# Deformable convolution in a hybrid block: gathering both neighbours of a sampling point from one long row instead of from a table of pairs

## The chip, the cores and the metric

The kernel runs on one core of a Trainium2 chip. The metric is the device time of one execution in microseconds (us). The core has the engines PE (TensorE), DVE (VectorE), ACT (ScalarE), POOL (GpSimd) and SP (SyncE, which here only issues DMAs). DMAs are issued from the instruction queues of SP, ACT and POOL, and an issue that waits holds up whatever stands behind it in that queue.

## The reference, cut to what matters

Four images of 64 x 64 tokens with 256 channels go through a deformable convolution, an additive attention and a routed feed-forward. The change is in the convolution's sampling. Every token has, for each of 8 groups of 32 channels and each of 9 taps, an offset; at that place the projected image `xp` is read by bilinear interpolation of four corners, weighted with a softmax mask, and summed over the taps.

```python
out = corner(x0i, y0i, (1.0 - fx) * (1.0 - fy))
out = out + corner(x0i + 1, y0i, fx * (1.0 - fy))
out = out + corner(x0i, y0i + 1, (1.0 - fx) * fy)
out = out + corner(x0i + 1, y0i + 1, fx * fy)
...
m = mask.reshape(N, H * W, G, P).transpose(0, 2, 1, 3).reshape(N * G, 1, H * W, P)
out = (samples * m).sum(-1)
...
return out @ out_w + out_b
```

## The kernel before

**Near and far tokens.** Most offsets are below 1 in size. For these tokens the sampling is a small dense product: a window of 5 x 5 weights for each token, written to DRAM, laid out as a band, turned on PE and multiplied with the projected rows of a tile of 16 x 8 tokens. Tokens with a larger offset are far tokens. Up to 128 of each image are listed (`list_tokens`) and computed exactly, one token to a partition, in `exact_rows`; an image with more than 128 would take another path (`sample_any`), which is not entered here.

**The table of pairs.** The projected rows are stored in DRAM as `xt_d`, one row of 256 channels for each position of the padded image (66 positions to a line). For the far tokens there is a second table `tab_d`: for each position and each group its 32 channels and the 32 channels of the next position, 64 numbers or 256 bytes. `pairs(i)` makes it: SP loads 128 positions with their right neighbours from `xt_d` (L471), ACT copies them into the order of groups (L476), ACT stores them (L477). It is called 33 times for each image, from `projection`, which evicts the projected rows on ACT (L458) and stores them (L460). Before all this, `zm`, a tile of zeros, is stored to the edges of `xt_d` and `tab_d` and to the four bands (L1625, L1630), and the pool of `zm` is closed before the next stage's tiles are allocated.

**Far tokens.** `exact_rows` is a generator. It fetches the offsets and masks of the listed tokens, computes the positions `ti` and the weights `wg`, and then, for each of 8 groups, issues 18 indirect DMAs on POOL (9 taps and 2 lines, L728), one for 128 tokens, two of them in each step. Then come one multiplication on DVE with the weights (L739, 1152 elements to a partition) and two reductions over the taps and corners (L742, 576 elements each). The tile `ga` has one buffer, so the next group's gathers wait for these reductions. The multiplication stands three steps after the last gather.

**Stages and order.** The first stage runs the convolution's offsets and weights for all four images, in 32 slabs of 512 tokens (`offsets_and_weights`); from slab 4 on, the sampling of image 0 (`sample_image(0, 3)`) goes along with it, and from slab 9 on its far tokens. A slab has five places at which sampling advances, by two, two, two, two and one steps. Then follow four rounds of preparation, feed-forward of the image before, and attention. Attention of image n has 256 steps, and at each of them the sampling of image n + 1 advances by one step, its far tokens too. One step of sampling is one entry of an order of 227: four transposes of weights (drained on DVE as `wt`, L817), a product (`ac`, L836) or an output (`xr`, L850), and at each new tile the loads of its rows and the addition `xr` on POOL (L806). `next(single)` adds to each step one piece of `exact_rows`. The order of the instructions on PE, DVE and POOL is that of the program where `keep` stands around them: here for the gathers, the multiplications and reductions, and the sampling's own instructions. In an attention step POOL also does `s12` (L1219) and `s3a` (L1221), whose sum DVE adds up at L1223 and L1226; there is one L1226 in each step.

Of the kernel before, what the change touches and what calls it, by code (L numbers as in the profile page):

```python
# [10 lines left out]
F32 = mybir.dt.float32  # L11
# [12 lines left out]
G, K2 = 8, 9  # L24
GP = G * K2
# [26 lines left out]
def layers_kernel(ctx: ExitStack, tc: tile.TileContext, a, out: bass.AP):  # L52
# [6 lines left out]
    def scratch(name, shape, dtype=F32):  # L59
        return [nc.dram_tensor(f"{name}{n}", shape, dtype, kind="Internal").ap() for n in range(NB)]  # L60

    tab_d = scratch("tab", [NPOS * G, 2 * CG])
    xt_d = scratch("xt", [NPOS, C])
    raw_d = scratch("raw", [L, 3 * GP])
    wc_d = scratch("wc", [L, RUN])
# [205 lines left out]
    def offsets_and_weights(images, slab):  # L271
# [163 lines left out]
        def image(at):  # L435
# [2 lines left out]
            xn = xns.pop(n)  # L438


            tabw = tab_d[n].rearrange("(q g) c -> q (g c)", g=G)

            def projection(s):

                for i in range(8 * s, 8 * s + 8 + s // 3):
                    if i == 8 * s + 4:
                        yield
                    o = PITCH + i * P
                    pm = S.a_m.tile([P, C], F32, tag="pm", name="pm")
                    for k in range(CC):  # L450
                        pe.matmul(
                            pm, xn[:, k].rearrange("p r q -> p (r q)")[:, o : o + P], inw[:, k, :],
                            start=(k == 0), stop=False,
                        )
                    m = o % PITCH
                    pe.matmul(pm, inside[:, m : m + P].bitcast(R32), inb2.bitcast(R32), start=False, stop=True)
                    xt = S.a_ld.tile([P, C], F32, tag="xt1", name="xt1", bufs=3)
                    nc.scalar.copy(xt, pm)  # L458
                    q0 = LEAD + PITCH + o
                    nc.scalar.dma_start(out=xt_d[n][q0 : q0 + P], in_=xt)  # L460
                    if i > 1:
                        pairs(i - 2)
                if s == 3:
                    pairs(i - 1)
                    pairs(i)

            def pairs(i):

                q0 = LEAD + 2 * PITCH + i * P
                x2 = S.a_ld.tile([P, 2, C], F32, tag="x2", name="x2", bufs=3)  # L470
                nc.sync.dma_start(  # L471
                    out=x2.rearrange("p c e -> p (c e)"),
                    in_=bass.AP(xt_d[n].tensor, xt_d[n].offset + q0 * C, [[C, P], [1, 2 * C]]),
                )
                tb = S.a_ld.tile([P, G, 2, CG], F32, tag="tb", name="tb", bufs=2)
                nc.scalar.copy(tb.rearrange("p g c e -> p c g e"), x2.rearrange("p c (g e) -> p c g e", g=G))  # L476
                nc.scalar.dma_start(out=tabw[q0 : q0 + P], in_=tb.rearrange("p g c e -> p (g c e)"))  # L477

            x1s, raws = {}, {}

# [184 lines left out]
    def exact_rows(n, uf, out_rows):  # L665

        ui = S.smp.tile([P, 1], I32, tag="ui", name="ui")  # L670
        nc.vector.tensor_copy(ui, uf)
        rf = S.smp.tile([P, 1], F32, tag="rf", name="rf")
        nc.vector.tensor_scalar(rf, uf, float(L - 1), None, ALU.min)
        ri = S.smp.tile([P, 4], I32, tag="rii", name="rii")
        nc.vector.tensor_copy(ri[:, 0:1], rf)
        nc.vector.tensor_scalar(rf, rf, float(n * L), None, ALU.add)
        nc.vector.tensor_copy(ri[:, 1:2], rf)
        nc.vector.tensor_scalar(ri[:, 2:3], ri[:, 0:1], W - 1, None, ALU.bitwise_and)
        nc.vector.tensor_scalar(ri[:, 3:4], ri[:, 0:1], 6, None, ALU.logical_shift_right)
# [24 lines left out]
        gt = S.dn.tile([P, 2, GP], F32, tag="gtt", name="gtt")  # L704
        nc.vector.tensor_copy(ti, pos)
        nc.vector.tensor_copy(fl, ti)
        nc.vector.tensor_tensor(gt, fl, pos, ALU.is_gt)
        nc.vector.tensor_sub(fl, fl, gt)
        nc.vector.tensor_sub(pos, pos, fl)
        nc.vector.scalar_tensor_tensor(gt[:, 0], fl[:, 1], float(PITCH), fl[:, 0], ALU.mult, ALU.add)  # L710
        nc.vector.scalar_tensor_tensor(gt[:, 0], gt[:, 0], float(G), gi, ALU.mult, ALU.add)
        nc.vector.tensor_scalar(gt[:, 1], gt[:, 0], float(G * PITCH), None, ALU.add)
        nc.vector.tensor_copy(ti, gt)
        yield True

        wg = S.dn.tile([P, GP, 2, 2], F32, tag="wg", name="wg")
        nc.vector.tensor_mul(fl[:, 1], rw[:, 2 * GP :], pos[:, 1])
        nc.vector.tensor_sub(fl[:, 0], rw[:, 2 * GP :], fl[:, 1])
        for dy in range(2):
            nc.vector.tensor_mul(wg[:, :, dy, 1], fl[:, dy], pos[:, 0])  # L720
            nc.vector.tensor_sub(wg[:, :, dy, 0], fl[:, dy], wg[:, :, dy, 1])

        so = S.dn.tile([P, G, CG], F32, tag="so", name="so")
        for g in range(G):
            ga = S.dn.tile([P, K2, 2, 2, CG], F32, tag="ga", name="ga")
            for s in range(K2):
                for dy in range(2):
                    keep(nc.gpsimd.indirect_dma_start(  # L728
                        out=ga[:, s, dy].rearrange("p c e -> p (c e)"), out_offset=None, in_=tab_d[n],
                        in_offset=bass.IndirectOffsetOnAxis(  # L730
                            ap=ti[:, dy, s * G + g : s * G + g + 1], axis=0
                        ),
                    ))
                yield
            yield
            yield True
            gf = ga.rearrange("p s r c e -> p s (r c) e")
            wv = wg.rearrange("p (s g) r (c o) -> p g s (r c) o", g=G, o=1)[:, g]
            keep(nc.vector.tensor_tensor(gf, gf, wv.to_broadcast([P, K2, 4, CG]), ALU.mult))  # L739
            for e in (slice(0, CG // 2), slice(CG // 2, CG)):  # L740
                yield True
                keep(nc.vector.tensor_reduce(  # L742
                    so[:, g, e], ga[..., e].rearrange("p s r c e -> p e (s r c)"), AX.X, ALU.add,
                ))
            yield
        pt = S.ps_m.tile([P, CC, P], F32, tag="pm", name="pso")
        sof = so.rearrange("p g e -> p (g e)")
# [870 lines left out]
    with scope(("one", 1, 0)):  # L1618
# [1 line left out]
        zm = S.one.tile([P, 2 * HALF * G], F32, name="zm")  # L1620
        nc.gpsimd.memset(zm, 0.0)
        for n in range(NB):
            for d, width in ((xt_d[n].rearrange("q c -> (q c)"), 1), (tab_d[n].rearrange("q c -> (q c)"), 2)):
                for o in (0, (LEAD + (H + 2) * PITCH) * C):
                    nc.scalar.dma_start(  # L1625
                        out=d[o * width : (o + edge) * width].rearrange("(p c) -> p c", p=P),
                        in_=zm[:, : edge * width // P],
                    )
        for slot in band_d:
            nc.scalar.dma_start(out=slot, in_=zm)  # L1630

# [91 lines left out]
```

## Time and profile before

| | |
|---|---|
| three runs | 9395.73, 9403.02 (median), 9404.38 us |
| the profiled execution | 9400.16 us, span 9398.4 us, granted PE clock 0.935 of full speed |
| busy in the span | PE 8133.7 us (87%), DVE 7332.7 (78%), ACT 7317.0 (78%), POOL 5164.1 (55%) |
| DMA traffic | 1282.92 MB, of these 54.39 MB by POOL's queue |
| attention passes (first to last L1133) | 1309 to 3011, 3375 to 5096, 5455 to 7175, 7503 to 9137 us |
| far tokens of image 0, first gather to last reduction | 392 to 845 us |

The profile is of one execution. A line of instructions is named by its line in the kernel. In a table of waits a row says who waited for whom, the sum in us, how often, and the longest. In the groups, the two numbers after the bar are the busy time in us and the mean duration of one instruction in ns; after the next bar stands the idle time of the engine before these instructions, with what ended most of it. A timeline row has the start, the duration, engine, line, operation and tiles. "SPq" and "ACTq" are the queues that issue DMAs.

### The profile page before, as it was taken

The page shows a single profiled execution, that of the slowest core. Times are in us where ns is not written, and L with a number is a line of the kernel's source. Part 1 is how long each engine was busy: PE and PEld are TensorE (multiplying, and loading weights), DVE is VectorE, ACT ScalarE, POOL GpSimd, SP SyncE. Part 2 cuts the span into 40 slices and gives each one's busy share as a digit, 9 for nine tenths or more (in the row PEclk, how much of TensorE's full clock was granted, in tenths as well). Part 3 has the DMA queues.
Part 4 walks back from the last instruction along what each step waited for, and adds up shares of the span by engine and source line. Part 5 has one row for each costly group of instructions (what it writes and reads, how often), then busy time and mean ns, then how long its engine had stood idle before and what let it go on. Part 6 is the DMA issues. An engine that isn't in the chain of part 4 may idle for free. (4 is left out here: it accounts for less than half of the span.)

```text
span 9398.4 us, 119496 instructions
## 1 busy us (share of the span) xinstructions
PE 8133.7 (87%) x35978; PEld 5811.0 (62%) x35978; DVE 7332.7 (78%) x13074; ACT 7317.0 (78%) x8469; POOL 5164.1 (55%) x3124
## 2 busy tenths in 40 slices
PE   5767679999998679999998679999996789999995
PEld 3545447777776357777776357777774456666663
DVE  6777759998987459888887469898987278888872
ACT  3333369999997369999997479999996399999982
POOL 0132057776665357776664367766663456666652
PEclk9888879999999799999998799999998899999997
DMA  5666665554442545554543455554433433333322
GB/s 169 192 187 199 197 204 138 140 136 135 134 135 85 181 133 139 135 136 137 147 119 106 168 132 138 137 144 139 137 112 106 160 116 106 105 102 104 102 85 82
DMA packets 1606155, 1282.92 MB, mean 137 GB/s; under 512 B 128834, under 2 KB 1412068, under 8 KB 1605476
## 3 DMA queue, kind: packets, MB, share of 16 engines
q1 hardware_dynamic: 1433316, 999.33, 36.5%
q10 hardware_dynamic: 139712, 221.19, 6.4%
q0 software_dynamic: 32448, 54.39, 3.9%
q8 instruction: 299, 4.90, 0.2%
q14 instruction: 380, 3.11, 0.1%
HBM read 979.60 MB, written 322.58 MB: 139 GB/s over the span
## 5 line engine op out<-in xcount | busy, mean ns | idle before, releaser
L1133 DVE TENSOR_TENSOR r<-nn,r 128x512 f32<-128x512 f32 x6144 | 4124.3, 687 | 819.0 <-PE nn L1110 605.3
L1219 POOL TENSOR_TENSOR r<-r 128x1024 f32<-128x1024 f32 x1024 | 2706.7, 2643 | 1797.2 <-DVE r L1133 1418.5
L1110 PE MATMUL nn<-qf,kf 128*128 128x512 f32 x8192 | 3227.6, 442 | 243.0 <-DVE r L1133 98.1
L1213 ACT ACTIVATE r<-d 128x1024 f32<-128x1024 f32 x3072 | 3063.7, 1015 | 361.5 <-DVE r L1223 194.4
L1215 ACT ACTIVATE r<-r 128x1024 f32<-128x1024 f32 x3072 | 3132.8, 1055 | 32.5
L1110 PE MATMUL d<-qf,kf 128*128 128x512 f32 x8192 | 2556.1, 414 | 130.9 <-DMA kf<-k 100.6
L1110 PEld LDWEIGHTS nn<-qf,kf 128*128 128x128 f32 x8192 | 1454.0, 188 | 1240.3 <-DVE r L1133 956.2
L1156 PE MATMUL pv<-v,et 128*128 128x257 f32 x8192 | 2134.7, 384 | 18.7 <-DVE acv L1178 18.7
L1110 PEld LDWEIGHTS d<-qf,kf 128*128 128x128 f32 x8192 | 1500.7, 189 | 469.0 <-ACT r L1213 114.1
L1156 PEld LDWEIGHTS pv<-v,et 128*128 128x128 f32 x8192 | 1530.2, 190 | 322.2 <-DVE acv L1178 25.1
L1221 POOL TENSOR_TENSOR r<-r 128x512 f32<-128x512 f32 x1024 | 1334.4, 1303 | 90.0 <-DVE r L1133 10.4
L1223 DVE TENSOR_TENSOR r<-r 128x512 f32<-128x512 f32 x1024 | 729.7, 713 | 19.3 <-POOL r L1219 18.9
L1226 DVE TENSOR_TENSOR et<-r 128x512 f32<-128x512 f32 x1024 | 717.3, 700 | 11.4 <-POOL r L1221 8.0
L728 POOL DMA_INDIRECT ga<-tab,tii x576 | 597.5, 1037 | 146.2 <-issue 114.3
L1140 ACT ACTIVATE et<-et 128x512 f32<-128x512 f32 x1024 | 628.8, 614 | 22.3 <-DVE et L1226 22.3
L806 POOL TENSOR_TENSOR xr<-xr,outb 128x256 f32<-128x256 f32 x128 | 104.0, 813 | 970.5 <-DMA xr<-in_x_dram 622.4
L813 PE MATMUL ptq<-ident,wq 128*120 128x128 f32 x2048 | 327.1, 288 | 149.4 <-DVE ac L836 73.8
L813 PEld LDWEIGHTS ptq<-ident,wq 128*120 128x120 f32 x2048 | 298.2, 185 | 213.0 <-DVE ac L836 63.4
L817 DVE COPY wt<-ptq 120x512 f32<-120x512 f32 x512 | 345.6, 681 | 1.6 <-PE ptq L813 1.5
L1536 POOL DMA_INDIRECT sort<-v,rif x128 | 125.9, 984 | 293.3 <-DVE rif L267 176.6
L476 ACT COPY tb<-x 128x512 f32<-128x512 f32 x132 | 80.3, 615 | 255.0 <-DMA tab<-tb 84.3
L267 PE MATMUL pc<-xn,diag 128*128 128x512 f32 x576 | 260.0, 606 | 8.3 <-ACT xn L413 8.3
(350 smaller groups left out, 5859.7 us busy)
## 6 DMA issues: line engine op xcount, KB each, us to landing
kf<-k SPq DMA_DIRECT2D x4096, 128.0 KB
wq<-band SPq DMA_DIRECT2D x256, 480.0 KB
x<-xt SPq DMA_DIRECT2D x132, 256.0 KB
tab<-tb ACTq DMA_DIRECT2D x132, 256.0 KB
v<-t SPq DMA_DIRECT2D x64, 512.0 KB
k<-kh ACTq DMA_DIRECT2D x128, 256.0 KB
qf<-q SPq DMA_DIRECT2D x256, 128.0 KB
qf<-n SPq DMA_DIRECT2D x256, 128.0 KB
```

What stands on the lines that cost most here:

```text
L728: keep(nc.gpsimd.indirect_dma_start(out=ga[:, s, dy].rearrange("p c e -> p (c e)"), out_offset=None, in_=tab_d[n], in_offset=bass.Indirect ...
L813: keep(nc.tensor.transpose(pt[:HALF, g, :], wq[:, 4 * f + g, :], ident))
L1110: keep(nc.tensor.matmul(dst, ks[b][:, blk, :].bitcast(R32), moving, start=(i == 0), stop=(i == len(blocks) - 1)))
L1133: keep(nc.vector.tensor_tensor(r[:, j, :], nn, r[:, j, :], ALU.mult))
L1140: keep(nc.scalar.activation(ets[b], ets[b], AF.Exp))
L1156: keep(nc.tensor.matmul(pv, ets[b0 + i][:, rows(j)], v[:, k0 + i, :], start=(i == 0), stop=(i == PVB - 1)))
L1213: keep(nc.scalar.activation(rs[b, p], ds.pop((b, p)), AF.Ln))
L1215: keep(nc.scalar.activation(rs[b, p], rs[b, p], AF.Exp, scale=-1.0))
L1219: keep(nc.gpsimd.tensor_tensor(rs[b, 1], rs[b, 1], rs[b, 2], ALU.add))
L1221: keep(nc.gpsimd.tensor_tensor(rs[b, 1][:, 0], rs[b, 1][:, 0], rs[b, 3][:, 0], ALU.add))
L1223: keep(nc.vector.tensor_add(rs[b, 1][:, 1], rs[b, 1][:, 1], rs[b, 3][:, 1]))
L1226: keep(nc.vector.tensor_add(et, rs[b, 1][:, 0], rs[b, 1][:, 1]))
```

## The change

The table of pairs goes: `tab_d`, its zero fills, `pairs` and its calls. `exact_rows` gathers from `xt_d`, seen as rows of 32 channels (position times 8 plus group, the same index as before). Each gather now takes 9 such rows in a run, 288 numbers or 1152 bytes to a token: the first is the group at the position, the last is the group at the next position, and the seven between belong to other groups and are not read. The tile `ga` holds three taps instead of nine, so each group is done in three chunks of six gathers; each chunk has one multiplication and one reduction, into one of three partial sums `so`, and at the end one reduction adds the three. The reduction and the first two gathers of the next chunk are in the same step; the multiplication stands two steps after the last gather. The weights `wg` are laid out by group.

```diff
-    tab_d = scratch("tab", [NPOS * G, 2 * CG])
...
-                    if i > 1:
-                        pairs(i - 2)
-                if s == 3:
-                    pairs(i - 1)
-                    pairs(i)
-
-            def pairs(i):
...
-        wg = S.dn.tile([P, GP, 2, 2], F32, tag="wg", name="wg")
+        wg = S.dn.tile([P, G, K2, 2, 2], F32, tag="wg", name="wg")
...
-        so = S.dn.tile([P, G, CG], F32, tag="so", name="so")
+        so = S.dn.tile([P, 3, C], F32, tag="so", name="so")
+        line = xt_d[n].rearrange("q (g e) -> (q g) e", g=G)
         for g in range(G):
-            ga = S.dn.tile([P, K2, 2, 2, CG], F32, tag="ga", name="ga")
-            for s in range(K2):
-                for dy in range(2):
-                    keep(nc.gpsimd.indirect_dma_start(
-                        out=ga[:, s, dy].rearrange("p c e -> p (c e)"), out_offset=None, in_=tab_d[n],
-                        in_offset=bass.IndirectOffsetOnAxis(
-                            ap=ti[:, dy, s * G + g : s * G + g + 1], axis=0
-                        ),
-                    ))
+            for c in range(3):
+                ga = S.dn.tile([P, 3, 2, G + 1, CG], F32, tag="ga", name="ga")
+                for s in range(3):
+                    for dy in range(2):
+                        j = (3 * c + s) * G + g
+                        keep(nc.gpsimd.indirect_dma_start(
+                            out=ga[:, s, dy].rearrange("p c e -> p (c e)"), out_offset=None, in_=line,
+                            in_offset=bass.IndirectOffsetOnAxis(ap=ti[:, dy, j : j + 1], axis=0),
+                        ))
+                    yield
                 yield
-            yield
-            yield True
-            gf = ga.rearrange("p s r c e -> p s (r c) e")
-            wv = wg.rearrange("p (s g) r (c o) -> p g s (r c) o", g=G, o=1)[:, g]
-            keep(nc.vector.tensor_tensor(gf, gf, wv.to_broadcast([P, K2, 4, CG]), ALU.mult))
-            for e in (slice(0, CG // 2), slice(CG // 2, CG)):
-                yield True
+                gf = ga.rearrange("p s r c e -> p (s r) c e")[:, :, :: G]
+                wv = wg[:, g, 3 * c : 3 * c + 3].rearrange("p s r (c o) -> p (s r) c o", o=1)
+                keep(nc.vector.tensor_tensor(gf, gf, wv.to_broadcast([P, 6, 2, CG]), ALU.mult))
+                yield
                 keep(nc.vector.tensor_reduce(
-                    so[:, g, e], ga[..., e].rearrange("p s r c e -> p e (s r c)"), AX.X, ALU.add,
+                    so[:, c, CG * g : CG * (g + 1)], gf.rearrange("p s c e -> p e s c"), AX.XY, ALU.add
                 ))
-            yield
+        yield
+        sof = S.dn.tile([P, C], F32, tag="sof", name="sof")
+        keep(nc.vector.tensor_reduce(sof, so.rearrange("p c e -> p e c"), AX.X, ALU.add))
+        yield
         pt = S.ps_m.tile([P, CC, P], F32, tag="pm", name="pso")
...
-            for d, width in ((xt_d[n].rearrange("q c -> (q c)"), 1), (tab_d[n].rearrange("q c -> (q c)"), 2)):
-                for o in (0, (LEAD + (H + 2) * PITCH) * C):
...
+            for o in (0, (LEAD + (H + 2) * PITCH) * C):
```

More of the change, by code (lines that the diff above doesn't have):

```diff
@@ L438, in image @@
             xn = xns.pop(n)
-            tabw = tab_d[n].rearrange("(q g) c -> q (g c)", g=G)
             def projection(s):
@@ L460, in projection @@
                     nc.scalar.dma_start(out=xt_d[n][q0 : q0 + P], in_=xt)
-                    if i > 1:
-                        pairs(i - 2)
-                if s == 3:
-                    pairs(i - 1)
-                    pairs(i)
-            def pairs(i):
[L469 to L477, printed above, removed]
             x1s, raws = {}, {}
@@ L714, in exact_rows, with by_tap @@
         yield True
-        wg = S.dn.tile([P, GP, 2, 2], F32, tag="wg", name="wg")
+        wg = S.dn.tile([P, G, K2, 2, 2], F32, tag="wg", name="wg")
         nc.vector.tensor_mul(fl[:, 1], rw[:, 2 * GP :], pos[:, 1])
         nc.vector.tensor_sub(fl[:, 0], rw[:, 2 * GP :], fl[:, 1])
+        def by_tap(t):
+            return t.rearrange("p (s g) -> p s g", g=G)
         for dy in range(2):
-            nc.vector.tensor_mul(wg[:, :, dy, 1], fl[:, dy], pos[:, 0])
-            nc.vector.tensor_sub(wg[:, :, dy, 0], fl[:, dy], wg[:, :, dy, 1])
@@ L723, in exact_rows @@
-        so = S.dn.tile([P, G, CG], F32, tag="so", name="so")
-        for g in range(G):
-            ga = S.dn.tile([P, K2, 2, 2, CG], F32, tag="ga", name="ga")
-            for s in range(K2):
-                for dy in range(2):
-                    keep(nc.gpsimd.indirect_dma_start(
-                        out=ga[:, s, dy].rearrange("p c e -> p (c e)"), out_offset=None, in_=tab_d[n],
-                        in_offset=bass.IndirectOffsetOnAxis(
-                            ap=ti[:, dy, s * G + g : s * G + g + 1], axis=0
-                        ),
-                    ))
-                yield
-            yield
-            yield True
-            gf = ga.rearrange("p s r c e -> p s (r c) e")
-            wv = wg.rearrange("p (s g) r (c o) -> p g s (r c) o", g=G, o=1)[:, g]
-            keep(nc.vector.tensor_tensor(gf, gf, wv.to_broadcast([P, K2, 4, CG]), ALU.mult))
-            for e in (slice(0, CG // 2), slice(CG // 2, CG)):
-                yield True
+            w1, w0 = (wg[:, :, :, dy, dx].rearrange("p g s -> p s g") for dx in (1, 0))
@@ new lines, in exact_rows @@
+            nc.vector.tensor_mul(w1, by_tap(fl[:, dy]), by_tap(pos[:, 0]))
+            nc.vector.tensor_sub(w0, by_tap(fl[:, dy]), w1)
+        so = S.dn.tile([P, 3, C], F32, tag="so", name="so")
+        line = xt_d[n].rearrange("q (g e) -> (q g) e", g=G)
+        for g in range(G):
+            for c in range(3):
[8 more added lines that the diff above has]
+                    yield
+                yield
+                gf = ga.rearrange("p s r c e -> p (s r) c e")[:, :, :: G]
+                wv = wg[:, g, 3 * c : 3 * c + 3].rearrange("p s r (c o) -> p (s r) c o", o=1)
+                keep(nc.vector.tensor_tensor(gf, gf, wv.to_broadcast([P, 6, 2, CG]), ALU.mult))
+                yield
@@ L742, in exact_rows @@
                 keep(nc.vector.tensor_reduce(
-                    so[:, g, e], ga[..., e].rearrange("p s r c e -> p e (s r c)"), AX.X, ALU.add,
+                    so[:, c, CG * g : CG * (g + 1)], gf.rearrange("p s c e -> p e s c"), AX.XY, ALU.add
                 ))
-            yield
+        yield
+        sof = S.dn.tile([P, C], F32, tag="sof", name="sof")
+        keep(nc.vector.tensor_reduce(sof, so.rearrange("p c e -> p e c"), AX.X, ALU.add))
+        yield
         pt = S.ps_m.tile([P, CC, P], F32, tag="pm", name="pso")
-        sof = so.rearrange("p g e -> p (g e)")
@@ L1622, in layers_kernel @@
         for n in range(NB):
-            for d, width in ((xt_d[n].rearrange("q c -> (q c)"), 1), (tab_d[n].rearrange("q c -> (q c)"), 2)):
-                for o in (0, (LEAD + (H + 2) * PITCH) * C):
[L1625 to L1628, printed above, removed]
+            for o in (0, (LEAD + (H + 2) * PITCH) * C):
+                nc.scalar.dma_start(
+                    out=xt_d[n].rearrange("q c -> (q c)")[o : o + edge].rearrange("(p c) -> p c", p=P),
+                    in_=zm[:, : edge // P],
+                )
         for slot in band_d:
```

## The prediction

> **What bounds the kernel now.** I read the page first: four long attention passes, where PE, DVE and ACT are all near 90%, and a first stage where none is.
>
> ```profile
> PE   5767679999998679999998679999996789999995
> DVE  6777759998987459888887469898987278888872
> ```
>
> Each digit is a slice of 235 us. The first five are the convolution stage. The sums by stage give the measure:
>
> ```profile
> 0.00:1250.00 1250.00, 842.70 (x3934) 582.88 (x3935) 913.28 (x1694) 461.49 (x689) 222.26 (x256) 0.82 0.62 191
> 1420.00:3040.00 1620.00, 1553.09 (x7360) 1153.72 (x7360) 1430.06 (x2403) 1502.04 (x1674) 1092.84 (x636) 0.99 0.47 128
> ```
>
> Stretch, length, then busy time of PE, PEld, DVE, ACT, POOL, clock, DMA share. In the first stage ACT is idle 63% of the time and DVE is the busiest; in attention DVE, ACT and PE share the bound. So ACT copies removed from the first stage are not worth their busy time; the question is who waits for them. Next the two groups that the change is about, and who holds SP's queue before 1250 us:
>
> ```profile
> L728 POOL DMA_INDIRECT ga<-tab,tii x576 | 597.5, 1037 | 146.2 <-issue 114.3
> L476 ACT COPY tb<-x 128x512 f32<-128x512 f32 x132 | 80.3, 615 | 255.0 <-DMA tab<-tb 84.3
> ...
> SPq L471 <- DMA xt<-xt: 191.8, 78, 11.2
> ...
> SPq L471 <- ACT tb L476: 40.0, 12, 9.6
> ```
>
> The pairs hold SP for 232 us and ACT idle for 255. Then what DVE waits for while image 0's far tokens are gathered (392 to 846 us):
>
> ```profile
> DVE raw L267 <- PE po L267: 42.4, 22, 5.0
> DVE ga L739 <- DMA ga<-tab,tii: 40.3, 6, 10.4
> DVE ga L739 <- issue: 15.6, 2, 9.0
> ```
>
> No ACT and no pair is in it: DVE waits for the gather itself, 55.9 us before its eight multiplications. In the three attentions the same line waits for nothing.
>
> **The change, part by part.** All sums are against the profiled execution, 9400.2 us (span 9398.4), 2.9 us below the median 9403.02. A difference under 0.2% (19 us) can't be told from none.
>
> *Start: -6 us.* The timeline of the first 50 us:
>
> ```profile
> 37.20 3.60 ACTq L1630 DMA_DIRECT2D band<-zm  x4
> 49.15 0.39 SPq L79 DMA_DIRECT2D inw<-in_L_conv_in_w_dram  x1
> ```
>
> From 29.1 us ACT issues 16 zero fills and the four bands; nothing runs until they have landed at 49.1 and free their buffer. 8 x 134 + 8 x 268 + 4 x 960 KB in 20 us; the 8 x 268 that go are 30% of it, 6.1 us. By issue time alone 8 x 0.47 = 3.8. I take 6; all that follows moves with it.
>
> *132 loads, ACT copies and stores of pairs: -9 us.* Busy time 80 us on ACT, 132 x 0.33 of issue there, but these count only where DVE or PE wait for ACT. From 120 us on, DVE waits for ACT 8.9 us in all (hat 5.1 + 1.2, red 1.5, omax 1.1); behind 0.6 us copies and waits for tab stores stand exactly these activations. So 9. Ends: 0 (they are late anyway) and 25 (PE's 27 us without a named releaser before wq and xw are late loads from SP's queue, and most of that goes too).
>
> *End of the stage: -3 us.* At 1113.9 DVE waits 3.2 us for a position count that is queued on PE behind projections which wait for ACT. The last pair's store is issued at 1149.97, while DVE ends the stage at 1150.1: beside it. 0 to 8.
>
> *DVE work: +5 us in image 0, +11 in the others.*
>
> ```profile
> L739 DVE TENSOR_TENSOR ga<-ga,wg 128x1152 f32<-128x1152 f32 x32 | 46.0, 1437 | 55.9 <-DMA ga<-tab,tii 40.3 <-issue 15.6
> L742 DVE TENSOR_REDUCE so<-ga 128x16 f32<-128x576 f32 x64 | 74.4, 1163 | 0.0
> ```
>
> Now 120.4 us / 4 = 30.1 per image. The multiplication becomes 24 of 384 elements; from 467 ns for 288 (w<-w,mxy) and 1359 for 1152 it is 170 + 1.03 x 384 = 0.57 us. The reduction becomes 24 of 384, all at strides; from 670 ns for 288 (red) and 1160 for 576 it is 0.83. One more sums 768 to 256: at those rates 1.5 to 1.7. 24 x 1.40 + 1.6 = 35.2: +5 per image. In image 0 DVE is the bound: 1 for 1. In attention a step (one sum, L1226, each) takes 6.76, 6.84 and 6.80 us while gathering (intervals of that line, 1420:2060, 3500:4130, 5580:6210) and 6.62, 6.58 and 6.59 after it: 0.21 x 112 steps = 23 us for 30.1 us of DVE, 0.77. 5 x 0.77 x 3 = 11. Ends: 0, if the smaller pieces fit the slack (a step without sampling is 6.24), and 24.
>
> *Gathers: +46 us, all in image 0.* Their number stays 576. A row of 1152 bytes is nowhere in the trace; the nearest, 1024 bytes (xre, L688), takes 0.99 us on POOL and lands in 3.7 to 4.0 us, against 0.95 and 3.4 / 4.0 / 7.9 for 256 bytes. I take no change; the ends are 0.3 us less on the landing and 3.9 more, the slowest gather of now. The Trainium skill (DMA: Bandwidth & Descriptors, Anatomy of one DMA) gives a gather a fixed 2.0 us and its bytes at 436 GB/s: 147 KB against 33 would be 0.26 us more, an estimate, 3 us over the short chunks below; no run here shows it yet.
>
> What moves is the wait. Now a group has 18 gathers in 9 steps, and its multiplication stands three steps after the last. Afterwards a chunk has 6 gathers in 3 steps; the multiplication stands two steps behind, and the next chunk's first gather, in the same step as the reduction, waits for it (one buffer ga). So there is a loop: reduction, gathers, landing, multiplication, with four steps from reduction to multiplication. DVE is in order: behind the waiting multiplication stand the drains wt, ac, xr that PE's next transposes wait for, and the convolution. How long are four steps? The drains tell, one a step:
>
> ```profile
> 924.28 0.28 DVE L836 COPY ac<-pmq 128x128 f32<-128x128 f32 x1
> 924.48 0.41 DVE L850 TENSOR_TENSOR xr<-poq,xr 128x256 f32<-128x256 f32 x1
> 927.17 0.29 DVE L836 COPY ac<-pmq 128x128 f32<-128x128 f32 x1
> 927.37 0.69 DVE L817 COPY wt<-ptq 120x512 f32<-120x512 f32 x1
> 933.19 1.28 DVE L817 COPY wt<-ptq 120x512 f32<-120x512 f32 x2
> 936.83 0.68 DVE L817 COPY wt<-ptq 120x512 f32<-120x512 f32 x1
> 937.43 0.28 DVE L836 COPY ac<-pmq 128x128 f32<-128x128 f32 x1
> 940.07 0.42 DVE L850 TENSOR_TENSOR xr<-poq,xr 128x256 f32<-128x256 f32 x1
> 954.92 0.28 DVE L836 COPY ac<-pmq 128x128 f32<-128x128 f32 x1
> ```
>
> Nine steps come in a burst of 16 us, then 15 us pass. From the nine starts four steps take 8.9, 9.4, 9.6, 10.0, 6.9, 21.0, 18.3, 20.7 and 18.6 us. The loop needs 0.83 + 5 x 1.38 (1.08 and 0.30 of issue) + 4.0 = 11.7. Chunks of 5 steps meet all nine phases, so 5 in 9, 13 of 24, are short, by 2.7 us on average: 36 us. That is the least: in POOL's order between the gathers also stands one addition xr (L806) in every 7 steps, which waits for its load, and POOL idled 207 us before 12 of them in this window. The most: each of the 24 waits as long as the eight do now, 55.9 / 8 = 7.0: 168. Neither is nearer; I take the middle, 102, +46 against 55.9. Ends: -20 and +112. SP without pairs loads xr earlier, which is why I don't go to the upper end.
>
> In attention steps are regular. The last gather of a group landed 13 us or more before its multiplication; one step less leaves 6. The first pair of a chunk now waits for the reduction, so the next s12 (L1219) starts about 1 us later in one step of five; its reader on DVE comes 2 us after it, so I take nothing.
>
> Sum: -6 - 9 - 3 + 5 + 11 + 46 = +44: 9444 against 9400.2, 9447 on the median.
>
> **The rivals.** *Faster:* the gathers find their time. With SP free of 232 us of pair waits, xr comes early, the additions no longer hold POOL, and the waits fall to the least, 36: the term is -20, the sum -22, and with 25 for late loads -38: 9365 to 9385. It decides below 58 us of waits in all (sum zero), 4.5 us for each short chunk. For it: 207 us of POOL idling before that addition. Against it: its load also waits for the store of the tile before, from the drain on DVE, which the pairs don't touch. *Long rows land late:* 24 multiplications each 3.9 us later add 94 us: about 9540. Against it the 1024-byte row. *The row is not one transfer:* if a row of 288 were split at the 32 elements that the index counts in, POOL would have nine times the descriptors; even at half the cost for each, 576 x 4 us of POOL are over 1000 us slower.
>
> **How the numbers follow.** Forecast 0.60: its own range is 9400 to 9520, of which 0.50 lies slower and 0.10 within 0.2%. Faster rival 0.28: 0.17 faster, 0.11 same (its smaller gains). Late rows 0.09 and split rows 0.03: slower. Faster 0.17, same 0.21, slower 0.62. All low ends together give 9348, all high ends 9542; together they are unlikely, so 9375 to 9525.
>
> **What would show it.** Right: the first input load at 43 us instead of 49; no x<-xt on SP; ga lands as before; DVE's wait before L739's successor in image 0 near 100 us, none in attention; image 0's last reduction later than now (845 us), the first attention starting some 30 us later than 1309, steps with gathers near 6.8. Wrong: waits below 58 us, gathers over 1.1 us on POOL, or a change within attention above 24 us.

## The result and the profile after

The changed kernel takes 9450.59 us (median of 5 runs, 9437.30 to 9454.67) against 9404.38 for the kernel before in the same runs: ratio 1.0044, 95% interval 1.0030 to 1.0059, or 46 us slower. The profiled execution took 9437.30 us with a span of 9435.6, 37 us above the profiled one of before. It is the fastest of the five, so the account of the waits below covers 37 of the 46 us.

The page's row of DVE and its DMA line, for the changed kernel (a digit is a slice of 236 us):

```profile
DVE  7766859999997459998987469998987378888872
...
DMA packets 1576204, 1277.57 MB, mean 135 GB/s; under 512 B 124482, under 2 KB 1407716, under 8 KB 1575524
```

The third and fourth digits, 7 and 7 before, are 6 and 6: the first stage has become emptier on its busiest engine, just where image 0's far tokens are gathered. The traffic as a whole is the same, since the longer rows add what the table saved. The sums by stretch, same columns and stretches as before:

```profile
0.00:1250.00 1250.00, 834.03 (x3897) 579.73 (x3898) 903.54 (x1707) 376.74 (x547) 211.01 (x252) 0.81 0.45 138
1420.00:3040.00 1620.00, 1564.97 (x7420) 1153.78 (x7418) 1464.94 (x2440) 1529.45 (x1702) 1115.90 (x650) 1.00 0.52 139
```

ACT lost 85 us of work in the first stage, and DVE did less in the same time, so the stage is stretched by waits. The start, from the timeline:

```profile
33.14 3.24 ACTq L1616 DMA_DIRECT2D band<-zm  x4
44.26 0.39 SPq L78 DMA_DIRECT2D inw<-in_L_conv_in_w_dram  x1
```

The first input load comes 4.9 us earlier. The groups of the gathers (before, then after) and of DVE's two steps:

```profile
L728 POOL DMA_INDIRECT ga<-tab,tii x576 | 597.5, 1037 | 146.2 <-issue 114.3 <-DVE so L742 6.9 <-DMA xr<-in_x_dram 0.3
```

```profile
L717 POOL DMA_INDIRECT ga<-xt,tii x576 | 621.0, 1078 | 381.2 <-DVE so L727 229.7 <-issue 106.3 <-DVE ac L823 24.0
...
L727 DVE TENSOR_REDUCE so<-ga 128x32 f32<-128x384 f32 x96 | 77.6, 808 | 0.0
...
L725 DVE TENSOR_TENSOR ga<-ga,wg 128x384 f32<-128x384 f32 x96 | 54.7, 570 | 120.3 <-DMA ga<-xt,tii 119.3 <-issue 1.0
```

POOL now idles 230 us for the reduction, where before it was 6.9, and DVE idles 120.3 us for gathers instead of 55.9. All of that DVE wait is in image 0. The table of waits while image 0's far tokens are gathered, now 381 to 921 us, and under it the row of before for PE's products (392 to 850 us):

```profile
POOL xr L793 <- DMA xr<-in_x_dram: 177.2, 15, 24.8
...
DVE ga L725 <- DMA ga<-xt,tii: 119.3, 16, 14.7
...
POOL ga L717 <- DVE so L727: 111.2, 15, 18.4
PE pmq L815 <- DVE wt L804: 58.9, 12, 12.2
```

```profile
PE pmq L828 <- DVE wt L817: 18.5, 11, 3.0
```

Read together they are one chain, which the experiments below test: POOL stands before the addition and before the reduction, so DVE stands before its multiplication, and PE's products stand for `wt`, which is queued on DVE behind that multiplication (its longest wait 12.2 us, before 3.0).

What one bad chunk looks like, in the timeline of POOL:

```profile
555.45 0.94 POOL L717 DMA_INDIRECT ga<-xt,tii  x1 [7.31 <-DVE so L727]
556.69 0.95 POOL L717 DMA_INDIRECT ga<-xt,tii  x1 [0.30 <-issue]
578.19 0.72 POOL L793 TENSOR_TENSOR xr<-xr,outb 128x256 f32<-128x256 f32 x1 [20.55 <-DMA xr<-in_x_dram]
579.06 0.96 POOL L717 DMA_INDIRECT ga<-xt,tii  x1
580.33 0.95 POOL L717 DMA_INDIRECT ga<-xt,tii  x1 [0.30 <-issue]
581.58 0.95 POOL L717 DMA_INDIRECT ga<-xt,tii  x1 [0.30 <-issue]
582.83 0.95 POOL L717 DMA_INDIRECT ga<-xt,tii  x1 [0.30 <-issue]
592.97 0.94 POOL L717 DMA_INDIRECT ga<-xt,tii  x1 [9.20 <-DVE so L727]
```

The chunk waits for the reduction, issues two gathers, stands 20.55 us behind the addition `xr` whose load is late, issues its other four, and DVE's multiplication of this chunk waits 14.7 us. Such an addition falls between the gathers of 7 of the 24 chunks. These 7 have 57.4 us of DVE's waits, 8.2 each; the other 17 have 62.9, 3.7 each.

By DVE's account up to the first attention (idle before each of its tiles, before against after), the stage grew from 1309.4 to 1342.4 us: gathers +64.4; the start (`inb`) -5.2; `hat`, `omax` and `red`, which wait for ACT, -8.5; `st`, `oh` and `fl`, all at the end of the stage, -11.7; `raw` -3.9; busy time -0.4; others -1.7. From there on the span is 4.2 us longer (8093.2 against 8089.0), and the three passes with sampling are together 1.9 us longer.

### The profile page after: what moved, and what is told of

It is laid out like the page before. It is cut to its first block, busy times and chain, and to the rows that moved or that the text cites. A ratio compares the mean times of both kernels' runs of the same rounds, so it can differ in the third digit from the quotient of the medians.

```text
span 9435.6 us, 119357 instructions
## 1 busy us (share of the span) xinstructions
PE 8158.0 (86%) x35978; PEld 5808.4 (62%) x35978; DVE 7386.4 (78%) x13174; ACT 7247.8 (77%) x8337; POOL 5176.9 (55%) x3124
## 5 line engine op out<-in xcount | busy, mean ns | idle before, releaser
L717 POOL DMA_INDIRECT ga<-xt,tii x576 | 621.0, 1078 | 381.2 <-DVE so L727 229.7
L1210 DVE TENSOR_TENSOR r<-r 128x512 f32<-128x512 f32 x1024 | 769.7, 752 | 18.4 <-POOL r L1206 18.1
L815 PE MATMUL pmq<-wt,xw 120*32 120x128 f32 x4096 | 176.5, 293 | 88.0 <-DVE wt L804 72.0
```

The lines of the kernel that those rows point to most:

```text
L717: keep(nc.gpsimd.indirect_dma_start(out=ga[:, s, dy].rearrange("p c e -> p (c e)"), out_offset=None, in_=line, in_offset=bass.IndirectOffs ...
L1210: keep(nc.vector.tensor_add(rs[b, 1][:, 1], rs[b, 1][:, 1], rs[b, 3][:, 1]))
```

## The experiments

Each difference is taken against the kernel before timed beside it, whose median lay between 9391 and 9404 us. A difference of two rows of the table carries both intervals, some 12 to 20 us together; a smaller one tells nothing. "Waits" are DVE's before the multiplications of image 0, "start" is that of the first attention, both from the one profiled execution of each kernel.

| kernel | median us | against before | interval of the ratio | waits us | start us |
|---|---|---|---|---|---|
| changed | 9450.59 | +46.2 | 1.0030 to 1.0059 | 120.3 | 1342.4 |
| two_buffers | 9419.73 | +17.2 | 1.0009 to 1.0027 | 90.7 | 1312.6 |
| late_add | 9342.27 | -60.3 | 0.9926 to 0.9952 | 64.0 | 1290.6 |
| before_chunks | 9481.38 | +78.8 | 1.0074 to 1.0101 | 127.3 | 1383.2 |
| before_no_table | 9353.37 | -49.2 | 0.9938 to 0.9964 | 38.8 | 1259.1 |
| loads_only | 9380.28 | -22.9 | 0.9967 to 0.9985 | 49.5 | 1281.9 |
| loads_nowait | 9367.40 | -23.9 | 0.9963 to 0.9983 | 37.8 | 1283.8 |
| short_rows | 9415.90 | +12.7 | 1.0006 to 1.0023 | 110.5 | 1328.4 |
| short_image0 | 9421.46 | +30.2 | 1.0021 to 1.0045 | 109.9 | 1332.6 |
| group_image0 | 9376.89 | -26.3 | 0.9961 to 0.9982 | 34.8 | 1275.9 |
| double_reduce | 9505.51 | +114.2 | 1.0109 to 1.0140 | 117.9 | 1353.9 |
| before_late | 9281.03 | -110.3 | 0.9867 to 0.9897 | 0.0 | 1254.1 |
| group_late | 9292.73 | -110.4 | 0.9865 to 0.9894 | 0.0 | 1242.0 |

### What makes the wait: the buffer or the addition

**two_buffers**

```diff
-                ga = S.dn.tile([P, 3, 2, G + 1, CG], F32, tag="ga", name="ga")
+                ga = S.dn.tile([P, 3, 2, G + 1, CG], F32, tag="ga", name="ga", bufs=1 if n else 2)
```

> The changed kernel, with two buffers for the gathered rows in image 0 (one in the other images). Theory (the wait is the loop through the one buffer: reduction, six gathers, landing, multiplication): the next chunk's gathers no longer wait for the reduction, POOL's 111 us of waits for it go, DVE's waits before the multiplications in image 0 fall from 120 us to about 30, and the time falls by about 75 us to near 9375. Rival (the additions xr hold POOL, the buffer only comes second): the seven chunks with an addition between their gathers keep their 57 us, the others lose at most half of their 63: the time falls by 30 us or less, to 9420. Rival (the landing of long rows): waits stay above 100 us and the time within 15 us of 9451.

29 us less than the changed kernel: the first rival's figure, not the theory's 75. As that rival said, the seven chunks with an addition keep most of their waits (52.4 of 57.4 us), and the others fall from 62.9 to 38.3. The waits in its gather window (379 to 896 us):

```profile
POOL xr L793 <- DMA xr<-in_x_dram: 239.6, 13, 27.6
...
DVE ga L725 <- DMA ga<-xt,tii: 80.4, 9, 14.7
```

No wait of POOL for the reduction is left, but what POOL saved there it now stands before the addition, 239.6 us instead of 177.2, and the longest wait of DVE is still 14.7. The addition is in POOL's order between the gathers, and a second buffer does not carry them past it.

**late_add**

```diff
-            keep(nc.gpsimd.tensor_add(xr, xr, outb))
...
+            if f == 1:
+                xr = held[i, "r"]
+                keep(nc.gpsimd.tensor_add(xr, xr, outb))
             pm = S.ps_m.tile([P, P], F32, tag="pm", name="pmq")
```

> The changed kernel, one buffer, with POOL's addition xr six steps later in a tile's seven (beside the second product instead of at the tile's start), so that its load has long landed. Theory (loop through one buffer): only the seven chunks of image 0 that have the addition between their gathers gain; their 57 us of waits fall to the mean of the others, 7 x 3.7 = 26: 30 us, 9420. Rival (the additions set the pace): POOL's 186 us of idling before them in the window go into earlier gathers everywhere, the waits fall below 60 us and the time by 60 us or more, below 9390. Rival (neither): within 10 us of 9451.

106 us less than the changed kernel, and 0.6% faster than the kernel before. Waits in the window 376 to 872 us:

```profile
POOL ga L717 <- DVE so L727: 194.4, 17, 18.3
...
DVE ga L725 <- DMA ga<-xt,tii: 64.0, 14, 8.7
```

The waits fell by 56 us, and the first attention starts 52 us earlier; so the addition did more than the theory's 30. Chunk by chunk, 35 us of this come from the 7 that had the addition between their gathers (57.4 to 22.5) and 21 from the other 17 (62.9 to 41.4), as if a held chunk also delayed those behind it. What is left is the loop itself: POOL waits 194.4 us for reductions, and no DVE wait is over 8.7. Both limits stand in a row, the addition first. The passes of attention are 10.7, 19.7 and 15.7 us shorter too. From 1420 to 2060 us POOL waited 17.2 us for the addition's load in the changed kernel and does not wait for it here; no run moves the addition in attention alone.

### What the chunks cost, whatever the rows

**before_chunks**

```diff
+            for c in range(3):
-            ga = S.dn.tile([P, K2, 2, 2, CG], F32, tag="ga", name="ga")
+                ga = S.dn.tile([P, 3, 2, 2, CG], F32, tag="ga", name="ga")
...
+        sof = S.dn.tile([P, C], F32, tag="sof", name="sof")
+        keep(nc.vector.tensor_reduce(sof, so.rearrange("p c e -> p e c"), AX.X, ALU.add))
```

> The kernel before, with its table and its rows of 256 bytes, but a group done in three chunks of six gathers with the changed kernel's steps, one small buffer, and the sum of three at the end. Theory (the chunks make the wait, whatever the rows): waits before the multiplications in image 0 as in the changed kernel, 105 to 120 us against 56; the time is the changed kernel's plus what the table costs (18 by the prediction, 30 by the account of DVE's waits in the first stage): 9470 to 9480. Rival (the long rows make the wait): waits near 60 us, the time within 15 us of 9404.

As the theory had it, and a little more: 79 us slower than before (67 to 77 expected), waits 127.3 us with rows of 256 bytes (105 to 120 expected). The chunks make the wait.

### What the table cost

**before_no_table**

```diff
-                    if i > 1:
-                        pairs(i - 2)
...
-                        out=ga[:, s, dy].rearrange("p c e -> p (c e)"), out_offset=None, in_=tab_d[n],
+                        out=ga[:, s, dy].rearrange("p c e -> p (c e)"), out_offset=None, in_=xt_d[n].rearrange("q (g e) -> (q g) e", g=G),
```

> The kernel before with its 18 gathers to a group, but no table: no zero fills of it, no loads, copies and stores of pairs. The gathers read 64 numbers at the same index from the projected rows, so that the right neighbour is left out (the next group stands in its place). It measures what the table costs by itself. Prediction: 6 + 9 + 3 = 18 us less than the kernel before, 9386. By the account of DVE's waits up to the first attention (inb 5, hat, omax and red 8.5, the end of the stage 12, raw and others 4): 30 us less, 9375. Rival (SP freed also brings xr earlier and shortens the gather waits): 45 us or more less, below 9360, with less than 36 us of waits before the multiplications.

49 us less: the rival's figure, not the prediction's 18. DVE's idle time up to the first attention falls from 374.7 to 325.0 us: gathers -17.1; ACT's (`hat`, `red`, `omax`) -8.6; the start -5.0; `st`, `oh` and `fl` -14.4; `raw` -6.3; others +1.7. The waits before the multiplications are 38.8 us, a little over the 36 that the rival named.

**loads_only**

```diff
-                tb = S.a_ld.tile([P, G, 2, CG], F32, tag="tb", name="tb", bufs=2)
-                nc.scalar.copy(tb.rearrange("p g c e -> p c g e"), x2.rearrange("p c (g e) -> p c g e", g=G))
-                nc.scalar.dma_start(out=tabw[q0 : q0 + P], in_=tb.rearrange("p g c e -> p (g c e)"))
```

(from the kernel before, with the gathers of before_no_table)

> The kernel before without the table's zero fills, copies and stores, but with the 132 loads of pairs on SP, which nobody reads; gathers of 64 numbers from the projected rows, the right neighbour left out. It splits the 50 us that the table cost. If the copies and stores on ACT cost them: as without the loads, 9353 to 9358, gather waits near 39 us. If SP, held by these loads until the projected rows are stored, costs the gather waits: these return to 56 us, and 9370. If SP costs the end of the stage too (st, oh, fl, raw: 21 us): 9390.

26 us of the 49 are the loads, more than the 17 of the middle case and less than the last; the intervals of the two runs leave 11 to 41. SP's queue before 1250 us still has its first row from them:

```profile
SPq L471 <- DMA xt<-xt: 165.1, 72, 9.2
```

The gather waits go back to 49.5 us, not quite 56, and `raw`, DVE's wait for PE, is 11.3 us longer than in before_no_table (107.6 against 96.3). `st`, `oh` and `fl` keep their gain, so these go with ACT's copies and stores.

**loads_nowait**

```diff
-                    in_=bass.AP(xt_d[n].tensor, xt_d[n].offset + q0 * C, [[C, P], [1, 2 * C]]),
+                    in_=bass.AP(x_d[n].tensor, x_d[n].offset + min(i * P, L - P - 1) * C, [[C, P], [1, 2 * C]]),
```

> As the run with only the 132 loads of pairs (9380), but each load reads 256 KB of the input x, which is there from the start, so that SP no longer stands until projected rows are stored; the traffic is the same. If holding SP costs the 27 us: 9353 to 9358, as without loads, gather waits near 39 us. If the traffic of 34 MB costs them (and by the same the 66 MB that long rows add): 9375 to 9382.

The time is that of loads_only, but the run does not separate the two causes. With nothing to wait for, 30 of the loads went ahead of the first input, and all 132 were issued by 319 us (the first row gives how many, how long each, and the first and last start):

```profile
L471 SPq DMA_DIRECT2D x<-in_x_dram x132: 327/328/1277, 4.2 to 319.2; - x132
...
20.51 41.29 SPq L471 DMA_DIRECT2D x<-in_x_dram  x30
...
61.92 0.38 SPq L79 DMA_DIRECT2D inw<-in_L_conv_in_w_dram  x1
```

The first input load starts at 61.9 instead of 44.4 us. Behind this delay of 17 us the gather window is 434 us long, as without loads (433, against 453 with loads that wait), and the waits are 37.8 us. But the first gather is at 398.9 us, after the last of the loads, so this window has neither a held SP nor the bytes: it moves 137 GB/s, as without loads (138), where loads_only moves 161. The loads beside the gathers cost them some 11 us of waits; whether by holding SP or by their bytes, no run here shows.

### What the long rows cost

**short_rows**

```diff
-                            out=ga[:, s, dy].rearrange("p c e -> p (c e)"), out_offset=None, in_=line,
+                            out=ga[:, s, dy, 0:2].rearrange("p c e -> p (c e)"), out_offset=None, in_=line,
...
-                gf = ga.rearrange("p s r c e -> p (s r) c e")[:, :, :: G]
+                gf = ga.rearrange("p s r c e -> p (s r) c e")[:, :, 0:2]
```

> The changed kernel with the same chunks and tiles, but gathering 64 numbers (256 bytes) of each row instead of 288, and using these; the right neighbour is left out (the next group stands in its place). Theory (the length of a row costs nothing that matters): waits 115 to 125 us, the time within 8 us of 9451. Rival (long rows land later: medians of 4.4 us against 4.0): 24 waits each 0.4 us shorter, 10 us: 9441. Rival (long rows hold up other transfers): waits below 100 us, 9430 or less.

33.5 us less than the changed kernel, outside what the theory (none) and the landing (10) allow. The waits did fall by the landing's share, 120.3 to 110.5, or 0.4 us for each of 24. The last rival's time came (21 or more less), but not the sign by which it was to be known, waits below 100. DVE's steps are as long as with long rows (555 and 793 ns in image 0 against 555 and 790).

**short_image0**

```diff
+                            out=ga[:, s, dy, 0 : (G + 1 if n else 2)].rearrange("p c e -> p (c e)"), out_offset=None, in_=line,
```

> The changed kernel, with rows of 64 numbers in image 0 alone (its right neighbour is left out) and the long rows in the three attentions. It says where the 35 us go that the rows of 64 gained in all images. If they are lost in the first stage: 9416 as with short rows everywhere. If half is lost in the attentions (their profiles differ by 14 us after the first attention's start, by 14 before it): 9437. If all of it is lost in the attentions: 9451.

The middle case: 16 of the 33.5 us go in the first stage, 17.5 in the three attentions. Either half alone is hardly clear of the intervals, but the profiles agree: the three passes add up to 5110 us in the changed kernel and in this one, and to 5094 with short rows everywhere. There the share of the DMA engines while gathering is 0.64 with long rows (1420 to 2060 us) and 0.56 with short ones, as before; a step (the first 140 of a pass) takes 6.81, 6.82 and 6.83 us against 6.80, 6.77 and 6.81. That the extra 66 MB hold up other transfers would fit this; no run shows it.

**group_image0**

```diff
+        taps = 3 if n else K2
+        chunks = K2 // taps
...
+                ga = S.dn.tile([P, taps, 2, G + 1, CG], F32, tag="ga", name="ga")
```

> The changed kernel, but in image 0, which shares the first stage, a group is done as before: 18 gathers (rows of 1152 bytes) into one tile of nine taps, one multiplication three steps after the last, two reductions. The other images keep the three chunks. Theory (all that the change loses is the chunks' loop in image 0; rows and attention cost nothing): waits before the multiplications fall from 120 to about 40 us as in the kernel without a table, the first attention starts near 1259 us, and the time is that kernel's, 9353, at most 8 us more. Rival (long rows land late or slow the gathers): waits above 55 us and 9370 or more. Rival (chunks also cost attention, 11 us by the prediction): 9364 with waits of 40.

It gains 72 us on the changed kernel and is faster than the one before (0.9972), 23 us above before_no_table. The waits are 34.8 us, so long rows cost the gathers nothing in this form; what DVE waits more is `raw`, 115.5 against 96.3 us, its wait for PE, and why that grows no run shows. The time fits the rival on the rows (9370 or more), but by another way than it said.

### What DVE's work costs in attention

**double_reduce**

```diff
                 keep(nc.vector.tensor_reduce(
                     so[:, c, CG * g : CG * (g + 1)], gf.rearrange("p s c e -> p e s c"), AX.XY, ALU.add
                 ))
+                keep(nc.vector.tensor_reduce(
+                    so[:, c, CG * g : CG * (g + 1)], gf.rearrange("p s c e -> p e s c"), AX.XY, ALU.add
+                ))
```

> The changed kernel with each of the 96 reductions of a chunk done twice: 19 us more DVE work in each image. By the prediction's rates (image 0: 1 for 1; attention: 0.77 for 1, three times): 19 + 45 = 64 us, 9515. Rival (in attention DVE's idle time, 164 us in a pass, takes extra work at regular steps): 19 us in image 0 and less than 10 in the attentions, 9470 to 9480, with attention passes of 1704 to 1707 us.

68 us more than the changed kernel, where the prediction's rates give 64: the rival falls. By the profile the passes are 23.7, 15.2 and 14.8 us longer (54 for three times 19.5 of work, 0.92 for 1), the first stage 11.5 us (for 19). So DVE's work is hardly hidden in attention.

### The addition out of the way

**before_late**: the edit of late_add, in the kernel before. **group_late**: the same edit in group_image0.

> The kernel before, table and all, with POOL's addition xr six steps later in a tile. It says whether that addition bound the kernel before too, and what the change is worth beside it. If it did: attention falls by 46 us and image 0's waits from 56 to below 20: 9403 - 46 - 40 = 9317, and the changed kernel with the same addition (9342) is still slower. If the addition only matters for the short loop of chunks: attention 46 less, waits still near 50, 9355, and the change would be a gain beside it.

> The kernel of the run before (image 0 by groups of 18 long rows, the others in chunks), with POOL's addition xr six steps later in a tile as well. If the two gains add: attention loses the 46 us that it lost with the later addition (11 + 20 + 16), and image 0's waits fall from about 40 to 15: 9353 - 46 - 25 = 9282. If the addition was the whole wait of image 0 and the chunks cost nothing any more once it is out of the way: no better than the chunks with the later addition in the first stage, 9342 - 20 = 9320.

Both take 1.2% less than the kernel before, and both have no wait before the multiplications. The addition bound the kernel before too: its waits of 55.9 us go entirely, and its passes fall from 1703, 1705 and 1703 us to 1683, 1684 and 1683. Beside this the changed kernel as it is (late_add) is 50 us behind: 64 us of waits are left in its loop, and its passes are 10.4, 0.3 and 6.0 us longer. With groups in image 0 the change is even: the first stage is 12.1 us shorter than with the table, the passes are 9.0, 5.7 and 5.2 us longer. The best two are level within their intervals, so beside the later addition the change, with groups kept in image 0, shows neither gain nor loss. The second case of group_late's expectation did not come (9320), the first nearly did (9282).

## Why the prediction was right, and where its steps were not

The forecast, 44 us slower by its sum, met 46; the waits in image 0 grew, as it said. But two of its terms were wrong, by 31 and 34 us in opposite directions, so that the sum came within 2 us is luck. The runs split the change into three: the table goes, -49.2 (before_no_table); then the chunks come, +61.9 (short_rows against it); then the long rows, +33.5. These were predicted as -18, +62 (46 + 5 + 11) and 0. The chunks' 62 met as a sum only: the waits before the multiplications grew by 71.7 us (38.8 to 110.5) where 46 were forecast, and the 11 in attention did not come. With the table still there the chunks cost 78.8, which the intervals do not tell from 61.9. (The ends of the prediction's terms come to about 9349 and 9540 on the median, where it wrote 9348 and 9542; nothing rests on that.)

- *Start, -6:* -5 (44.26 us against 49.15, predicted 43). Right.
- *Pairs on ACT, -9:* -8.5 by the four activations that it named. Right in its own terms; what the pairs cost the gathers, the next step but one, was not in it.
- *End of the stage, -3, at most -8:* -11.7. The step looked at one position count on PE; that wait fell from 3.2 to 0.5 us, and two more went nearly or wholly: that of `st` for the load `v` (5.3 to 0.8) and that of `oh` for PE (5.0 to 0).
- *SP freed:* the prediction gave this only to the Faster rival, and kept it as a reason not to go to the upper end. 17.1 us of gather waits do go with the table, and 10.7 of them come back with the loads alone (loads_only), be it by the hold on SP or by the bytes. With this and the end of the stage the table is worth 49 and not 18: this is the first step that failed, a term put at nothing.
- *DVE work:* in image 0 +5 predicted, +3.6 measured (29.7 us for `ga` and `so` before, 33.3 for these and `sof` after). By the groups it is 34.1 us for an image ((54.7 + 77.6 + 4.1) / 4) where 35.2 were forecast: the two rates were right (0.57 against 0.57, 0.81 against 0.83), the last sum takes 1.02 us and not 1.5 to 1.7. In the attentions, +11: the passes grew by 1.9. The rate 0.77 was not the fault: double_reduce gives 0.92. The first 140 steps of a pass, which hold all its gathers, did grow, by 0.042, 0.014 and 0.030 us each, 12 us in all; the 111 after them became shorter by 0.049, 0.027 and 0.019, some 10 us. What shortens these is open. With the addition late, the changed kernel's passes are 17 us longer than the old one's (late_add against before_late), chunks and long rows together.
- *Gather waits, 102 against 55.9:* 120.3, inside the ends 36 and 168. Both mechanisms were in the step, the loop and the addition in POOL's order; but the addition was put beside the loop as a reason for the middle, and it is the larger: 56 us of 120.3 go with it, and 30 with the buffer. The growth was 64.4 where 46 were forecast. Waits of 24 x 2.7 us remain when it is out of the way, which lies between the step's "least" of 36 and the middle.
- *Long rows, 0:* POOL's 1.08 us (1.08 too in before_chunks, with short rows) and the landing, 4.4 us in the median against 4.0, lie within the step's bounds, and so do the landing's 10 us. But the step priced a gather alone. The rows cost 33.5 us, about half of it in attention where no multiplication waits for a gather: this is the second step that failed. How the rows cost that is open. The Trainium skill (DMA: Bandwidth & Descriptors, Anatomy of one DMA) gave 0.26 us, an estimate, for the longer rows of one gather; measured over all gathers that the traces time, the median landing is 4.0 us with short rows and 4.4 with long (before_chunks and the changed kernel), 0.4 more.
- *The signs:* the first input load at 44.26 us, no load of pairs on SP, image 0's last reduction at 920.6 us (before 845), the first attention 33 us later (forecast some 30), steps with gathers 6.81 to 6.83 us (near 6.8), no wait for gathers in attention. They came, with waits of 120 us where "near 100" was named and gathers that land 0.4 us later; none of the signs named as wrong did.
- *The rivals:* Faster has its condition refuted, 120 us against 58, though 17 us of gather waits do go with the table. Long rows do not land 3.9 us later. Rows are not split: 1078 ns on POOL against 1037.

## What to carry to other kernels

When a queue is in order, list everything that stands in it between the work that you time: here an addition that waited for a load held the gathers, and moving it six steps was worth 110 us in the kernel before and 106 in the changed one, more than the whole change in either direction. Give an edit's traffic and freed queue slots a price of their own, beyond the instructions that wait for them, and measure the parts: a total that agrees can hide two terms that don't. When a test takes a wait away, check in its trace that it leaves the rest in place: loads_nowait moved its loads out of the stretch that it was to test. A smaller buffer that must be emptied before it is filled again can turn a few long waits into many short ones: here 8 waits, 56 us together, became 17, 120 us together, in the first stage, and none in attention.

## What had not been expected of the hardware

The same instruction with the same shapes takes different times in different kernels. The division in attention (128 x 256, `t`), in the groups of the kernel before and of the changed one, and in the changed one's last pass alone (7579 to 9173 us), where no sampling runs beside it:

```profile
L1188 DVE SCALAR_TENSOR_TENSOR t<-acv,es,tr 128x256 f32<-128x256 f32 x128 | 108.5, 848 | 4.6
```

```profile
L1175 DVE SCALAR_TENSOR_TENSOR t<-acv,es,tr 128x256 f32<-128x256 f32 x128 | 129.7, 1013 | 4.5
...
L1175 DVE SCALAR_TENSOR_TENSOR t<-acv,es,tr 128x256 f32<-128x256 f32 x28 | 13.6, 485 | 1.0
```

848 and 1013 ns on average, 726 in before_late; 485 ns in the last pass, and that in every kernel. The addition `s3b` (128 x 512) goes the same way: 713, 752 and 691 ns, and 681 or 682 in the last pass. So it is neither the build nor the length of the rows (988 ns with short rows everywhere). The traces show what ends a slow one. One slow division of the changed kernel and what POOL does beside it:

```profile
1624.08 2.37 POOL L1206 TENSOR_TENSOR r<-r 128x1024 f32<-128x1024 f32 x1
...
1624.28 2.45 DVE L1175 SCALAR_TENSOR_TENSOR t<-acv,es,tr 128x256 f32<-128x256 f32 x1
```

It starts while POOL's `s12` runs and ends 0.28 us after it. In the kernel before and in the changed one, every division of more than 515 ns (71 of 128 and 72 of 128) starts while an element-wise operation of POOL runs (`s12`, `s3a` or `xr`). All but three of these end 0.28 to 0.30 us after that operation; the three start beside `xr` and outlast the `s12` behind it. Of the 20 and 18 that start beside no such operation, gathers or not, none takes more than 486 ns. So busy time on DVE is here in part a wait for POOL, and how long an instruction takes depends on where it falls in POOL's order. Why it falls worse in the kernels with chunks was not tried. And a second buffer in image 0 alone, which is gone before attention, came with 6.9 and 5.8 us more in the first two passes; that is one profile, and nothing explains it. A pass of before_no_table differs from the same pass of the kernel before by up to 9 us, so one pass of one profile tells little.
